# Layer 2 of a decoder: softmax sums and mask in three bf16 parts instead of fp32

## The chip, the cores and the metric

The kernel runs on one core of one Trainium2 chip. It is one launch that computes a whole four-layer decoder. The metric is device time in microseconds (us); lower is better. A core has a matmul engine (TensorE, PE in the profile, with its weight loads listed apart as PEld), VectorE (DVE), ScalarE (ACT), GpSimd (POOL), and SyncE (SP), whose queue issues nearly all DMAs here. Matmuls read their two operands from SBUF and write to PSUM[...].

## What is computed

The reference takes x of 4 x 512 tokens with 128 features and a context of 4 x 77 tokens, and applies four layers of self attention, cross attention and a feed-forward block, each as `x = x + block(layernorm(x))`. The change touches two blocks of layer 2:

```python
# cross attention (4 heads of 32), context tokens masked
logits = where(mask, MASK_FILL, q @ k.T)        # MASK_FILL = -2.3819763e38
# "ffn": attention of 16 heads of 64 whose values and outputs are mixtures of 8 experts
gv, go = gate(x, Wsel_v), gate(x, Wsel_o)       # sigmoid, the 2 best of 8 experts
v   = einsum('bsd,bhse,hedp->bhsp', x, gv, Wv)
att = softmax(einsum('bhsp,bhtp->bhst', q, k) / sqrt(64))
o   = einsum('bhst,bhtp->bhsp', att, v)
out = einsum('bhsp,bhse,hepd->bsd', o, go, Wo)
```

followed by a dense block with two layer norms. All inputs are fp32.

## The kernel before, in words

Matmuls are written through `dot` (line 421), which issues one product for each pair it is given and adds them in PSUM. An fp32 product of up to 512 columns stands in the trace as two MATMUL instructions, a bf16 product as one. `tt` (line 432) is VectorE's two-operand operation; everything that goes through it has that line in the profile, so such groups are told apart by tile names.

**The attention of layer 2's third block** is `l2_ffn`. It makes 32 passes, one for each of 4 batches and 8 pairs of heads, over PSUM tag `mm` with 7 banks. A pass t is three lists of steps:

- `attend(t)`: four row tiles of scores (`score`), each exponentiated on ScalarE with the row sums accumulated into `den` (128 x 4 x 2: query row, row tile, head of the pair); the exponentials turned by TensorE, 8 transposes for each row tile (`turn`, line 1795); then `turn_sums`, which inverts `den` on VectorE (line 1800), turns it with four fp32 transposes (line 1803) into a 2 x 512 PSUM tile and copies that on ScalarE to `dT` (line 1805); then `values`, 16 half-width instructions of the attention times v (line 1812) into `po`, and one product of `pick` (2 x 128, row h is one in the 64 columns of head h) with `dT`, which spreads the inverted sums over 128 partitions, and `po` is scaled with it on VectorE (the group `mm<-oT,mm`).
- `finish(t-1)`: the output experts of the pass before (groups `og<-mm,c` on VectorE and line 1845 on TensorE).
- `project(t+1)`: queries, keys, their rotation, and gated values (groups `roped`, `rot`, `gvx`) for the next pass.

`emit` puts the steps of the second and third list between those of the first, in proportion to the weights that stand beside the steps of `attend`. The passes are in turn woven with a second chain by `weave`: in rounds 0 to 14 the layer-2 attention, cross attention and gates of batches 2 and 3 (one step of the chain for every 3.3 steps of the passes), in rounds 15 to 30 the dense block of batches 0 and 1 (one for every 9), at the end that of batch 2. This program order is what the source gives; the framework that builds the kernel then orders each engine's queue by its own estimates, so a VectorE instruction may stand some places earlier or later in its queue than in the source. Waits between engines are semaphores that it sets.

**The cross attention of layer 2** is `l2_context` (once) and `l2_xattn` (for each batch). `l2_context` loads one row of the mask, and makes `fill`, a row of 4 x 77 fp32 values that are zero or MASK_FILL (lines 1542 to 1549). `score(j)` in `l2_xattn` adds two products in PSUM: queries times keys, 308 columns, and a product of a row of ones (1 x 128) with `fill`, repeated for four heads, which adds the mask to all 128 rows (lines 1611 to 1615). There are 16 of these, four for each batch. Those of batches 0 and 1 run beside the second half of layer 1's experts, those of batches 2 and 3 beside the passes of `l2_ffn`.

**Two helpers that are there already** and that the change calls: `in_three` (line 1281) splits an fp32 tile into three bf16 parts with four VectorE operations, the last of which gives the third part; `turned3` (line 1291) turns such a tile with four bf16 transposes and copies it on ScalarE. Layer 0 uses both for its own sums, with 48 columns, and has similar operations with 12 columns at lines 1151 to 1163.

Of the kernel before, what the change touches and what calls it, by code (L numbers as in the profile page):

```python
# [13 lines left out]
F32 = mybir.dt.float32  # L14
BF16 = mybir.dt.bfloat16
I32 = mybir.dt.int32
U8 = mybir.dt.uint8
AF = mybir.ActivationFunctionType
ALU = mybir.AluOpType
# [3 lines left out]
P = 128  # L23
B, S, D = 4, 512, 128
NT = B * S // P
TB = S // P
L = 77
BIG = 1.0e30
PAD = -3.0e38
FILL = -2.3819763e38  # L30
# [36 lines left out]
def rep(v):  # L67
    v = np.asarray(v).reshape(1, -1)
    return np.broadcast_to(v, (P, v.shape[1]))
# [35 lines left out]
def in_parts(a, n):  # L105

    out = []
    for _ in range(n):
        out.append(a.astype(ml_dtypes.bfloat16))
        a = a - out[-1].astype(np.float32)  # L110
    return out
# [19 lines left out]
def pack_all(inp):  # L131
    f32 = np.float32
# [3 lines left out]
    p = packs["const"] = Pack()  # L136
    p.add("tri8", rep((np.arange(8)[None, :] < np.arange(8)[:, None]).astype(f32)))
    p.add("tri4", rep((np.arange(4)[None, :] < np.arange(4)[:, None]).astype(f32)))
    p.add("place", ((np.arange(TB)[None, :, None] * P + np.arange(P)[:, None, None]) * 4 + np.arange(4)).astype(f32))
    p.add("slot1", rep((np.arange(32) * CAP + 1).astype(f32)))  # L140
    p.add("upper", (np.arange(P)[:, None] < np.arange(P)[None, :]).astype(f32))
    hd = np.arange(P) // 8
# [8 lines left out]
    one, zero = np.ones((32, S), f32), np.zeros((32, S), f32)  # L151
# [4 lines left out]
    p = packs["l0_attn.qk"] = Pack()  # L156
# [9 lines left out]
    p = packs["l0_attn.vo"] = Pack()  # L166
# [9 lines left out]
    p = packs["s1"] = Pack()  # L176
# [15 lines left out]
    p = packs["s2"] = Pack()  # L192
# [19 lines left out]
    p = packs["s3"] = Pack()  # L212
# [3 lines left out]
    turn = np.concatenate([np.arange(16, 32), np.arange(16)])  # L216
# [20 lines left out]
    for hp in range(8):  # L237
        h = slice(2 * hp, 2 * hp + 2)
        p = packs[f"l2_ffn.qkv{hp}"] = Pack()
# [3 lines left out]
        p = packs[f"l2_ffn.o{hp}"] = Pack()  # L243
        p.add("o", inp["L2_ffn_Wo"][h].transpose(0, 2, 1, 3).reshape(P, 8, D))
    p = packs["s4"] = Pack()
# [18 lines left out]
    p = packs["s5"] = Pack()  # L264
    p.add("gate_bias", rep(inp["L3_ffn_bias"]))
    p = packs["s5.gate"] = Pack()
# [23 lines left out]
class Net:  # L290
# [7 lines left out]
    def __init__(self, ctx, tc, packs, dram, feed):  # L298
        self.tc, self.nc = tc, tc.nc
        self.packs, self.dram = packs, dram  # L300
        self.feed, self.loaded = feed, []
        self.stay = {}
        self.turn = 0
        self.last = []
        self.chunks, self.sums = {}, {}
        nc = self.nc
        pool = lambda name, bufs, **kw: ctx.enter_context(tc.tile_pool(name=name, bufs=bufs, **kw))
        self.keep = pool("keep", 1)
        self.wpool = pool("weights", self.SLOTS)
        self.small = pool("small", 4)  # L310
        self.away = pool("away", 1, space=bass.MemoryType.DRAM)

        k = self.keep
        self.x = k.tile([P, NT, D], F32, name="x")
        self.xn = k.tile([P, NT, D], F32, name="xn")
        self.xT = k.tile([P, NT * P], F32, name="xT")
        xin = dram["x"].rearrange("(t p) d -> p t d", p=P)
        fetch = lambda b: nc.sync.dma_start(self.x[:, TB * b : TB * b + TB, :], xin[:, TB * b : TB * b + TB, :])
        fetch(0)
        self.want(0)  # L320
        self.const = self.load("const", k, "const")
        self.want(1)
        for b in range(1, B):
            fetch(b)
        self.ident = k.tile([P, P], F32, name="ident")
        make_identity(nc, self.ident)
        self.ones = k.tile([P, P], F32, name="ones")
        nc.gpsimd.memset(self.ones, 1.0)
        self.identb = k.tile([P, P], BF16, name="identb")
        nc.vector.tensor_copy(self.identb, self.ident)  # L330

        self.causal = k.tile([P, P], BF16, name="causal")
        nc.gpsimd.memset(self.causal, 0.0)
        nc.gpsimd.affine_select(
            out=self.causal, in_=self.causal, pattern=[[-1, P]], compare_op=ALU.is_ge,
            fill=-BIG, base=0, channel_multiplier=1,
        )
# [1194 lines left out]
    def l2_context(self, W, pool, work):  # L1532


        nc = self.nc
        H = 4
        one = lambda shape, name: pool.tile(shape, F32, tag=name, name=name, bufs=1)
        temp = lambda shape, name: work.tile(shape, F32, tag=name, name=name, bufs=2)
        s1 = one([P, 1], "s1")
        nc.vector.tensor_scalar(s1, W["rms"], 1.0, None, ALU.add)  # L1540

        mask8 = pool.tile([1, B * L], U8, name="mask8", bufs=1)
        nc.sync.dma_start(mask8, self.dram["mask"][0:1, :])
        fill = one([1, B * L], "fill")
        for a in "q", "qr":
            nc.vector.tensor_scalar(W[a], W[a], s1, None, ALU.mult)
        yield
        nc.vector.tensor_copy(fill, mask8)
        nc.vector.tensor_scalar(fill, fill, 1.0, -FILL, ALU.subtract, ALU.mult)
        ctx = self.const["ctx"].rearrange("l (b d) -> l b d", b=B)  # L1550
        mv = self.moments(lambda b: ctx[:, b, :], B, self.small, "rc")[:L]
        yield
        ms, rc = one([L, B], "ms"), one([L, B], "rc")
        self.tt(ms, mv[:, :, 0], mv[:, :, 0], ALU.mult)
        self.tt(ms, ms, mv[:, :, 1], ALU.add)
        self.rsqrt(rc, ms, 1e-6)
        yield
        cn = temp([L, B, D], "q")
        self.tt(cn, ctx, rc.unsqueeze(2).to_broadcast([L, B, D]), ALU.mult)
        yield  # L1560
        pt = self.sm()
        for b in range(B):
            nc.tensor.transpose(pt[:, b * L : b * L + L], cn[:, b, :], self.ident[:L, :L])
        cT = temp([P, B * L], "k")
        nc.vector.tensor_scalar(cT, pt[:, : B * L], s1, None, ALU.mult)
        yield
        t1, t2 = temp([P, B, L], "v"), temp([P, B, L], "e4")
        view = lambda ps: ps[:, : B * L].rearrange("p (b l) -> p b l", b=B)
        kb, vo = one([P, B, H, L], "kb"), one([L, H, B, D], "vo")
        self.x2 = kb, vo, fill  # L1570
        nc.gpsimd.memset(kb, 0.0)
        for t, w, c in ((t1, "k", "cosk"), (t2, "kr", "sink")):
            ps = self.sm()
            self.dot(ps[:, : B * L], (W[w], cT))
            self.tt(t, view(ps), W[c].unsqueeze(1).to_broadcast([P, B, L]), ALU.mult)
            yield
        for h in range(H):
            r = slice(32 * h, 32 * h + 32)
            self.tt(kb[r, :, h, :], t1[r], t2[r], ALU.add)
        yield  # L1580
        pv = self.sm()
        self.dot(pv[:, : B * L], (W["v"], cT))
        vT = temp([P, B * L], "q")
        nc.scalar.copy(vT, pv[:, : B * L])
        yield
        for h in range(H):
            r = slice(32 * h, 32 * h + 32)
            po = self.sm((P, B, D))
            for b in range(B):
                self.dot(po[:L, b, :], (vT[r, b * L : b * L + L], W["o"][r, :]))  # L1590
            self.move(vo[:, h], po[:L])
            yield

    def l2_xattn(self, b, W, pool, n):
        nc = self.nc
        H = 4
# [12 lines left out]
        def score(j):  # L1609
            s = self.sm((P, H, L))  # L1610
            self.dot(
                s,
                (q[:, j * P : j * P + P], kb[:, b]),
                (self.ones[0:1, :], fill[:, b * L : b * L + L].unsqueeze(1).to_broadcast([1, H, L])),
            )
            return self.less_maxima(s, H, pool, 2 * n)

# [75 lines left out]
    def l2_ffn(self, pool, gv, y, away, passes, feed, wants):  # L1693
# [5 lines left out]
        E = 8  # L1699
        n = len(passes)  # L1700

        pick = pool.tile([2, 2, 64], F32, name="pick")
        nc.gpsimd.tensor_copy(pick, self.ident[:2, :2].unsqueeze(2).to_broadcast([2, 2, 64]))

        other = pool.tile([P, 2, S], F32, name="rot")
        nc.gpsimd.memset(other, 0.0)
# [55 lines left out]
        def attend(t):  # L1762
# [28 lines left out]
            def turn(i):  # L1791
                for hl in range(2):
                    p = self.mm((P, TB, P))
                    for j in range(TB):
                        nc.tensor.transpose(p[:, j, :], es[i][hl][:, j * P : j * P + P], self.ident)  # L1795
                    nc.scalar.copy(eT[hl][:, :, i * P : i * P + P], p)  # L1796

            def turn_sums():
                spread(0)
                nc.vector.reciprocal(den, den)  # L1800
                p = self.mm((2, S))
                for i in range(TB):
                    nc.tensor.transpose(p[:, i * P : i * P + P], den[:, i, :], self.ident)
                m["dT"] = pool.tile([2, S], F32, tag="dT", name="dT")
                nc.scalar.copy(m["dT"], p)

            def values():
                spread(1)
# [14 lines left out]

            return [
                (lambda: score(0, 1), 4), (lambda: turn(0), 1), (lambda: score(2, 3), 1), (lambda: turn(1), 2),
                (lambda: turn(2), 2), (lambda: turn(3), 2), (turn_sums, 1), (values, 4),
            ]

        def finish(t):
# [546 lines left out]
```

## Time and profile before

| what | value |
|---|---|
| median of 3 runs | 2305.12 us (2304.5 to 2309.32) |
| the profiled execution | 2308.67 us |
| its span in the profile | 2306.8 us |
| PE busy, of the span | 94% |
| DVE busy, of the span | 69% |
| ACT busy, of the span | 45% |
| POOL busy, of the span | 24% |
| stretch of the 32 passes | from about 913 to 1917 us |
| granted clock of TensorE in that stretch | 1.00 |

The profiled execution is 3.55 us above the median. Its span leaves 1.9 us of the execution outside. Matmul records overlap each other[...]: a 512-column fp32 instruction is shown as 592 ns long, but the next starts 429 ns after it. What an instruction costs TensorE is therefore read from starts, not from its duration. A timeline line joins instructions of one group that follow each other; the cost of such a line is the start of the next line less its own.

### The profile page before, as it was taken

What the parts mean: (1) busy time and instruction counts of PE and PEld (TensorE: products, weight loads), DVE (VectorE), ACT (ScalarE), POOL (GpSimd) and SP (SyncE); (2) the same over time, 40 slices, a digit from 0 to 9 for tenths busy, and PEclk for the clock granted to TensorE, in tenths of its full rate; (3) what the DMA queues carried; (4) which work ended last, traced back from release to release, by engine and by line L of the source; (5) the groups of instructions that cost most, each with busy time, mean ns of one, the idle gap of its engine ahead of it and who ended that gap; (6) DMA issues with size and microseconds to landing.
All of it is one profiled execution on the core that took longest, in us unless ns stands there. A gap on an engine that the chain in (4) does not pass through costs nothing. (4 is left out here: it accounts for less than half of the span.)

```text
span 2306.8 us, 28326 instructions
## 1 busy us (share of the span) xinstructions
PE 2164.1 (94%) x9154; PEld 1142.8 (50%) x9154; DVE 1600.5 (69%) x4027; ACT 1027.8 (45%) x2102; POOL 556.6 (24%) x693
## 2 busy tenths in 40 slices
PE   6999899999999998999999999999999999498878
PEld 3566556554545553444444444444444444465553
DVE  6666576566675779777967696767776765686636
ACT  4555446444325462544444344444444444165432
POOL 1000001000000002333323333333333332335552
PEclk8988899999999999999999999999999999799779
DMA  6321134153453344233333344333333334200022
GB/s 165 99 61 43 45 108 132 51 141 104 110 148 90 90 103 117 59 94 94 92 85 82 87 113 108 103 103 94 103 103 94 82 99 101 92 1 6 1 71 75
DMA packets 81774, 204.72 MB, mean 89 GB/s; under 512 B 18799, under 2 KB 37551, under 8 KB 81371
## 3 DMA queue, kind: packets, MB, share of 16 engines
q1 hardware_dynamic: 78058, 198.99, 32.2%
q0 software_dynamic: 3568, 3.93, 0.6%
q8 instruction: 72, 1.18, 0.2%
q14 instruction: 76, 0.61, 0.1%
HBM read 173.94 MB, written 23.40 MB: 86 GB/s over the span
## 5 line engine op out<-in xcount | busy, mean ns | idle before, releaser
L1756 POOL TENSOR_TENSOR gvx<-gvx 128x512 f32<-128x512 f32 (+1 forms) x256 | 259.8, 1015 | 583.7 <-DVE gvx L432 528.6
L421 PE MATMUL f<-xT,w_l_ffn 128*128 128x512 f32 (+1 forms) x768 | 367.9, 601 | 1.2 <-ACT h L1001 0.7
L1876 ACT ACTIVATE at_e<-mm,at_m 128x512 f32<-128x512 f32 x256 | 172.8, 685 | 215.3 <-DVE at_m L1874 209.6
L421 PE MATMUL mm<-w_l_ffn_qkv,xT 128*128 128x512 f32 x512 | 265.5, 603 | 3.3 <-DVE roped L1727 1.7
L1845 PE MATMUL mm<-og,w_l_ffn_o 128*128 128x512 f32 x512 | 264.6, 600 | 0.0
L432 DVE TENSOR_TENSOR h<-h,f 128x512 f32<-128x512 f32 (+1 forms) x192 | 131.3, 685 | 136.1 <-PE f L421 110.3
L1001 ACT ACTIVATE h<-f 128x512 f32<-128x512 f32 x189 | 112.4, 596 | 249.7 <-PE f L421 217.2
L421 PEld LDWEIGHTS f<-xT,w_l_ffn 128*128 128x128 f32 (+1 forms) x768 | 139.5, 191 | 149.0 <-issue 126.1
L1009 PE MATMUL acc<-h,w_l_ffn 128*128 128x512 f32 x378 | 193.4, 596 | 3.5 <-DVE h L432 2.9
L432 DVE TENSOR_TENSOR og<-mm,c 128x512 f32<-128x512 f32 x256 | 175.8, 688 | 29.0 <-PE mm L1845 27.6
L432 DVE TENSOR_TENSOR gvx<-mm,gv 128x512 f32<-128x512 f32 x256 | 174.3, 683 | 23.6 <-PE mm L421 18.9
L1796 ACT COPY eT<-mm 128x512 f32<-128x512 f32 x256 | 137.5, 595 | 73.3 <-PE mm L1795 73.0
L1874 DVE TENSOR_REDUCE at_m<-mm 128x1 f32<-128x512 f32 x256 | 161.2, 683 | 8.9 <-PE mm L421 7.2
L1795 PEld LDWEIGHTS mm<-ident,at_e 128*128 128x128 f32 x1024 | 120.1, 141 | 67.0 <-issue 49.5
L1845 PEld LDWEIGHTS mm<-og,w_l_ffn_o 128*128 128x128 f32 x512 | 89.4, 191 | 97.0 <-issue 85.3
L1795 PE MATMUL mm<-ident,at_e 128*128 128x128 f32 x1024 | 134.1, 273 | 2.6 <-ACT at_e L1876 2.6
L421 PE MATMUL mm<-roped 64*128 64x512 f32 x512 | 133.4, 623 | 1.5 <-DVE roped L432 1.0
L421 PEld LDWEIGHTS mm<-w_l_ffn_qkv,xT 128*128 128x128 f32 x512 | 86.7, 190 | 91.9 <-issue 69.4
L1139 DVE TENSOR_REDUCE m<-mm 128x1 f32<-128x512 f32 (+3 forms) x176 | 105.3, 637 | 35.5 <-PE mm L1135 34.7
L1812 PE MATMUL mm<-eT,v 128*64 128x512 f32 x512 | 119.5, 599 | 0.0
L1009 PEld LDWEIGHTS acc<-h,w_l_ffn 128*128 128x128 f32 x378 | 70.9, 191 | 92.9 <-issue 66.9
L432 DVE TENSOR_TENSOR h<-h,c 128x512 f32<-128x512 f32 x160 | 111.1, 700 | 3.9 <-DMA c<-l_ffn_w 1.1
(457 smaller groups left out, 3646.3 us busy)
## 6 DMA issues: line engine op xcount, KB each, us to landing
c<-gates SPq DMA_DIRECT2D x256, 256.0 KB
c<-l_ffn_w SPq DMA_DIRECT2D x96, 384.0 KB
w_l_ffn<-in_l_ffn SPq DMA_DIRECT2D x26, 576.0 KB
w_l_ffn_qkv<-in_l_ffn_qkv SPq DMA_DIRECT2D x16, 640.0 KB
w_l_ffn_o<-in_l_ffn_o SPq DMA_DIRECT2D x16, 512.0 KB
rot<-qk SPq DMA_DIRECT2D x128, 64.0 KB
k_parts<-k SPq DMA_DIRECT2D x12, 384.0 KB
qs<-q_parts SPq DMA_DIRECT2D x48, 96.0 KB
```

The costliest lines, as they stand in the source:

```text
L421: self.nc.tensor.matmul(out, lhsT=lhsT, rhs=rhs, start=i == 0, stop=i == len(pairs) - 1)
L432: self.nc.vector.tensor_tensor(out, a, b, op)
L1001: nc.scalar.activation(h, pg, AF.Silu)
L1009: nc.tensor.matmul(acc["t"], lhsT=W["d" + u], rhs=h, start=i == 0, stop=i == n - 1)
L1139: nc.vector.tensor_reduce(m[:, i, h0 : h0 + per], ps, AX.X, ALU.max, negate=True)
L1756: nc.gpsimd.tensor_tensor(x[:, :, :m], x[:, :, :m], x[:, :, m : 2 * m], ALU.add)
L1795: nc.tensor.transpose(p[:, j, :], es[i][hl][:, j * P : j * P + P], self.ident)
L1796: nc.scalar.copy(eT[hl][:, :, i * P : i * P + P], p)
L1812: nc.tensor.matmul(po[64 * hl : 64 * hl + 64, :], lhsT=m["v"][:, j, hl, :], rhs=eT[hl][:, j, :], start=j == 0, stop=j == TB - 1,)
L1845: nc.tensor.matmul(acc, lhsT=W["o"][:, (e - 1) * D : e * D], rhs=hs.pop(e - 1), start=e == 1, stop=e == E)
L1874: nc.vector.tensor_reduce(m, s, AX.X, ALU.max, negate=True)
L1876: nc.scalar.activation(e[:, :n], s, AF.Exp, bias=m, accum_out=den)
```

## The change

The softmax sums of `l2_ffn` are inverted in a step of their own, `invert`, that stands between `turn(1)` and `turn(2)` with weight 0, and there they are also split into three bf16 parts with `in_three`. `turn_sums` turns the parts with `turned3`: four bf16 transposes of 6 columns in place of four fp32 ones of 2 columns, and a 6 x 512 copy in place of a 2 x 512 one. `pick` becomes a bf16 tile of 6 rows, each head's row three times, so that the spreading product is one bf16 product over 6 rows that adds the three parts. In the cross attention MASK_FILL is split into three bf16 parts on the host (one more column, `fill`, in the `const` pack), the mask is loaded in three rows, and the mask's product is a bf16 product over 3 rows of ones.

```diff
@@ pack_all
+    parts = in_parts(np.array([FILL], f32), 3)
+    p.add("fill", -np.concatenate(parts).astype(f32).reshape(3, 1))
@@ Net.__init__
+        self.onesb = k.tile([3, P], BF16, name="onesb")
+        nc.gpsimd.memset(self.onesb, 1.0)
@@ l2_context
-        mask8 = pool.tile([1, B * L], U8, name="mask8", bufs=1)
-        nc.sync.dma_start(mask8, self.dram["mask"][0:1, :])
-        fill = one([1, B * L], "fill")
+        mask8 = pool.tile([3, B * L], U8, name="mask8", bufs=1)
+        nc.sync.dma_start(mask8, self.dram["mask"][0:3, :])
+        mask, fill = one([3, B * L], "mask"), pool.tile([3, B * L], BF16, name="fill", bufs=1)
...
-        nc.vector.tensor_copy(fill, mask8)
-        nc.vector.tensor_scalar(fill, fill, 1.0, -FILL, ALU.subtract, ALU.mult)
+        nc.vector.tensor_copy(mask, mask8)
+        nc.vector.tensor_scalar(fill, mask, 1.0, self.const["fill"], ALU.subtract, ALU.mult)
@@ l2_xattn, score
-                (self.ones[0:1, :], fill[:, b * L : b * L + L].unsqueeze(1).to_broadcast([1, H, L])),
+                (self.onesb[0:3, :], fill[:, b * L : b * L + L].unsqueeze(1).to_broadcast([3, H, L])),
@@ l2_ffn
-        pick = pool.tile([2, 2, 64], F32, name="pick")
-        nc.gpsimd.tensor_copy(pick, self.ident[:2, :2].unsqueeze(2).to_broadcast([2, 2, 64]))
+        rows = pool.tile([6, 2], F32, name="own_rows")
+        pick = pool.tile([6, 2, 64], BF16, name="pick")
+        nc.gpsimd.tensor_tensor(rows, self.ident[:6, 0:2], self.ident[:6, 2:4], ALU.add)
+        nc.gpsimd.tensor_tensor(rows, rows, self.ident[:6, 4:6], ALU.add)
+        nc.gpsimd.tensor_copy(pick, rows.unsqueeze(2).to_broadcast([6, 2, 64]))
@@ l2_ffn, attend
+            def invert():
+
+                nc.vector.reciprocal(den, den)
+                m["d3"] = pool.tile([P, TB, 3, 2], BF16, tag="d3", name="d3")
+                self.in_three(m["d3"], den, pool, "d_rest")
+
             def turn_sums():
                 spread(0)
-                nc.vector.reciprocal(den, den)
-                p = self.mm((2, S))
-                for i in range(TB):
-                    nc.tensor.transpose(p[:, i * P : i * P + P], den[:, i, :], self.ident)
-                m["dT"] = pool.tile([2, S], F32, tag="dT", name="dT")
-                nc.scalar.copy(m["dT"], p)
+                m["dT"] = self.turned3(m.pop("d3"), pool)
...
-                (lambda: turn(2), 2), (lambda: turn(3), 2), (turn_sums, 1), (values, 4),
+                (invert, 0), (lambda: turn(2), 2), (lambda: turn(3), 2), (turn_sums, 1), (values, 4),
```

The helpers that it calls:

```python
    def in_three(self, out, w, pool, tag):
        nc = self.nc
        r, n = w.shape[1], w.shape[2]
        rest = pool.tile([P, r, n], F32, tag=tag, name=tag)
        nc.vector.tensor_copy(out[:, :, 0, :], w)
        self.tt(rest, w, out[:, :, 0, :], ALU.subtract)
        nc.vector.tensor_copy(out[:, :, 1, :], rest)
        self.tt(out[:, :, 2, :], rest, out[:, :, 1, :], ALU.subtract)

    def turned3(self, parts, pool):
        nc = self.nc
        n = 3 * parts.shape[3]
        t = self.bank("mm", [n, S], BF16)
        for j in range(TB):
            nc.tensor.transpose(t[:, j * P : j * P + P], parts[:, j].rearrange("p k n -> p (k n)"), self.identb)
        out = pool.tile([n, S], BF16, tag=f"turned{n}", name="turned", bufs=1)
        nc.scalar.copy(out, t)
        return out
```

## The prediction

> **What bounds the kernel now.** I read the page's busy shares first, then the same shares stretch by stretch, then TensorE's timeline inside one pass, since only starts tell its cost.
>
> ```profile
> PE 2164.1 (94%) x9154; PEld 1142.8 (50%) x9154; DVE 1600.5 (69%) x4027; ACT 1027.8 (45%) x2102; POOL 556.6 (24%) x693
> ...
> core 0: us, PE busy (x) PEld busy (x) DVE busy (x) ACT busy (x) POOL busy (x), PEclk, DMA share, GB/s
> 1403.00:1489.00 86.00, 86.00 (x326) 39.10 (x322) 63.79 (x114) 36.68 (x87) 29.35 (x36) 1.00 0.41 111
> 913.00:1403.00 490.00, 480.50 (x1880) 229.87 (x1878) 376.01 (x726) 218.04 (x500) 172.54 (x208) 1.00 0.35 91
> 690.00:913.00 223.00, 216.89 (x706) 109.78 (x705) 162.07 (x434) 104.49 (x164) 15.06 (x24) 0.99 0.37 97
> ```
>
> Three clean passes (1403 to 1489) have PE busy in every microsecond, DVE in 74%. In the passes woven with other work PE is at 98%, in the stretch with layer 1's last experts at 97%, at full clock. PE's queue sets the time in both places that the change touches. The waits of the clean passes say the same:
>
> ```profile
> engine line waited for: us in total, times, longest us
> ...
> DVE mm L432 <- PE mm L421: 15.3, 3, 5.2
> ```
>
> Once a pass DVE stands about 5 us at `mm<-oT,mm` for the product with `pick`: DVE waits for PE there. The timeline of PE (start, length, then the group; cost is start to start):
>
> ```profile
> 1196.49 1.02 PE L421 MATMUL mm<-w_l_ffn_qkv,xT 128*128 128x512 f32 x2
> 1197.35 1.02 PE L421 MATMUL s<-q,k 128*128 128x512 f32 x2
> 1198.21 0.60 PE L1803 MATMUL mm<-ident,den 128*2 128x128 f32 x4
> 1198.65 1.02 PE L1845 MATMUL mm<-og,w_l_ffn_o 128*128 128x512 f32 x2
> 1199.60 3.65 PE L1812 MATMUL mm<-eT,v 128*64 128x512 f32 x16
> 1203.19 1.12 PE L421 MATMUL mm<-dT,pick 2*128 2x512 f32 x2
> 1204.24 1.12 PE L421 MATMUL mm<-w_l_ffn_qkv,xT 128*128 128x512 f32 x2
> 1205.20 1.02 PE L1845 MATMUL mm<-og,w_l_ffn_o 128*128 128x512 f32 x2
> ```
>
> A full-array fp32 product costs 0.86 us (1196.49 to 1197.35). The product with `pick` costs 1.05, and the one after it 0.96: whenever the shape in use changes between full array, few rows and few columns, the instruction before is followed 0.09 us late (L1845 before L1812: 0.95), and the next fp32 product loses 0.10. The fp32 transposes with 2 columns cost 0.44 together and show no such loss.
>
> **What the Trainium skill says.** "TensorE: Matmul & The Clock Gate", section "Wait — 56ns, not 53.3ns?", gives 55.6 and 215.7 ns from start to start for warm bf16 matmuls of 128 and 512 columns; the lines below agree. "TensorEngine Tiling (Array Packing)", section "Key Properties", says that changing the tiling mode drains the array, which fits the 0.09 us; its section "Restrictions" says that column tiling disables the fp32 transpose mode, which fits that 2-column fp32 transposes pay no drain, and warns that bf16 ones may.
>
> **The change on PE, part by part.** What bf16 costs is shown in layer 0 and at the end of layer 3:
>
> ```profile
> 104.37 1.02 PE L421 MATMUL mm<-turned,pick 48*128 48x512 bf16 x4 [0.70 <-ACT turned L1299]
> 105.32 0.39 PE L1161 MATMUL mm<-identb,d 128*12 128x128 bf16 x4
> 105.64 0.39 PE L1132 MATMUL mm<-ks,qs 81*128 81x512 bf16 x1
> ...
> 2293.42 0.60 PE L421 MATMUL s<-w3T,pick 96*128 96x512 bf16 x2
> 2293.86 1.88 PE L421 MATMUL f<-xT,w_l_ffn 128*128 128x512 f32 x4
> ...
> 779.62 0.68 PE L421 MATMUL s<-kb,q 128*128 128x308 f32 x2
> 780.24 0.78 PE L421 MATMUL s<-fill,ones 1*128 1x308 f32 x2
> 780.95 0.79 PE L421 MATMUL s<-kb,q 128*128 128x308 f32 x2
> ```
>
> *Spreading product, 32 times.* Two bf16 products with 96 rows cost 0.44 (2293.42 to 2293.86), so 0.215 to 0.22 each, and going from fp32 to bf16 costs nothing in itself. Four with 48 rows cost 0.95: four times 0.215 and one drain of 0.09. Now: 0.09 before, 1.05, 0.10 on the next = 1.24. After, with 6 rows: 0.09 + 0.215 + 0.09 + 0.10 = 0.495. Gain 0.745, times 32 = 23.8 us. If 6 rows drained nothing, 0.215 would be left and the gain 32.8; no row shows so few rows in bf16, and the two fp32 products with 1 and 2 rows both pay, so I take 23.8.
>
> *Transposes, 32 x 4.* Now 0.44. The nearest row is the 12-column one: 0.32 for four (105.32 to 105.64), that is 4 x 0.056 and one drain of 0.09. Entering costs another 0.09, and the fp32 product after it, L1845, 0.10: 0.51. That is a loss of 0.07, 2.2 us in all. If 6 bf16 columns change no mode it is 0.22, a gain of 0.22 or 7.0 us. I take the loss, since the 12-column row drains and the fp32 exemption doesn't carry over.
>
> *Mask products, 16.* Now 0.71 (780.24 to 780.95), with the 0.09 of the drain into it and 0.10 on the next besides. At the bf16 rate 308 columns are 0.13, with the drain out of it 0.22; what lies on both sides stays. Gain 0.49, times 16 = 7.8 us, half of it beside layer 1's experts at 97% PE. Bounds: nothing there if DVE holds that stage (4 us), 9 if no drain is paid.
>
> Sum on PE: -23.8 + 2.2 - 7.8 = -29.4 us.
>
> **What it adds elsewhere.** `in_three` is four DVE operations a pass. The nearest rows:
>
> ```profile
> L432 DVE TENSOR_TENSOR d_rest<-m,d x16: 168/172/177, 40.4 to 255.4; 128x16 f32<-128x16 f32 x16
> L1153 DVE CAST d<-d_rest x16: 172/182/560, 40.6 to 256.0; 128x16 bf16<-128x16 f32 x16
> ```
>
> So 4 x 0.18 = 0.7 us a pass, 23 us in all, hidden by the 5 us that DVE stands once a pass; if that cover were gone it would cost all of it. The reciprocal already stands right behind the last exponential of its pass (0.12 us after it in clean passes), so `invert` adds hardly any wait. Queued behind it stand `rot`, `gvx`, `roped` and `og`. The tightest is the `og` that in one clean pass ran at 1452.45 and was used at 1455.79: 2.66 us of slack, of which 0.7 goes. The new hand-over is the third part, which must be ready for the transposes: in the built program it stands about eight places behind the reciprocal, after that `og`, so at about 1453.9, and PE reached the transposes at 1455.36. Some 1.1 us, allowing for the weight load ahead of them, is left in a clean pass, less where the woven chain puts more before it.
>
> The step `invert` also lengthens a pass from 27 steps to 28, so the woven chain advances 4% sooner. The order of the built program shows PE's queue in clean passes otherwise unchanged, some chain work a few places earlier, and ScalarE with four more table loads, between the sigmoids of the gates and the exponentials. One takes 1.283 us in this trace; the skill's "ScalarE activation tables: per-element evaluation and per-set limits", section "What a function is on this engine", has the same figure. ScalarE is busy 45%, and the exponentials are ready 2 us or more ahead of their transposes in 95 of 100 cases. For table loads, late parts and reshuffled chain I put 1.5 us, between -6 and +12: PE's idle gaps in the passes sum to some 20 us now, in a few pieces of up to 3 us, and a new order can mend or make such pieces.
>
> At nothing: the copy of 6 rows on ScalarE (12 rows took 574 ns as 2 rows do), the three GpSimd operations for `pick` (once, 40 us before use; 1.5 us if uncovered), the memset, the cast and scaling of the mask (0.3 us each as before; DVE works partitions in parallel), two more mask rows in one DMA, and one column more in 2244 of the `const` load, for which one DVE instruction waits 0.5 us at the start (under 0.05 us). SP's queue keeps its DMAs.
>
> Total: -29.4 + 1.5 = -28 us. The profiled execution would go from 2308.67 to about 2281; the median stood 3.55 us below it, so 2305.1 - 28 = 2277 us.
>
> **Rivals.** *A, small bf16 shapes cost no drain:* for it, the skill ties drains to tiling modes and nothing here shows 6 columns; against it, 12 columns and 48 rows both drain. Transposes gain 7.0 instead of losing 2.2, and the product may gain more: 2268, down to 2259 at most. *B, DVE and the reshuffled queues take back a good part:* DVE is at 77% in the woven stretch (376 of 490 us) and the change shortens PE's side while adding to DVE's. If half of the 32 passes lose 0.7 us, 11 us come back: about 2289. *C, slower:* the third part comes after PE reaches the transposes. PE takes its queue in order, so `values` would stand as well. It decides when PE waits over 29.4/32 = 0.92 us in every pass, so the part must come 2 us later than I place it (the 1.1 us of cover and 0.92); if it came 3 us later, 32 waits of 1.9 us would give 2338. Against it: DVE catches up before that in clean passes. *D, no gain:* a bf16 product of 6 rows is paced like fp32; the 0.95 for four of 48 rows speaks against it. Then some 2303.
>
> **How the numbers follow.** Forecast 0.68 (2271 to 2284), A 0.14, B 0.13, C 0.02, D 0.03. The predicted time is the forecast's, 2277. The range 2263 to 2290 takes in most of A and half of B. This kernel's measurement can tell about 0.2%, 4.6 us, from no change: faster 0.95, same 0.03, slower 0.02.
>
> **What would show it.** In the profile after: the line with `turned` and `pick` followed by the next product 0.3 us later (0.215 means A), that next product at 0.96; the four transposes of `d` at 0.32 with 0.09 before (0.22 means A); a clean pass 0.67 us shorter than 28.46 (1403.42 to 1431.88, from one product with `pick` to the next); mask products at 0.22; DVE's wait at `mm<-oT,mm` about 1.3 us shorter. PE waiting at the transposes for `d` would show C or B. The prediction is wrong if clean passes don't shorten, or if idle gaps of PE in the woven passes grow by more than 10 us.

## The result, and the profile after

| | before | after |
|---|---|---|
| median of 4 runs each, same chip | 2304.81 us (2299.01 to 2309.32) | 2279.88 us (2274.62 to 2285.02) |
| ratio after / before | | 0.9892, 95% interval 0.9871 to 0.9914 |
| the profiled execution | 2308.67 us | 2274.62 us |
| its span in the profile | 2306.8 us | 2272.5 us |
| first product of the mask, from the start of the span | 776.2 us | 764.8 us |
| from there to the end | 1530.6 us | 1507.8 us |

The kernel became 24.9 us faster (the interval makes that 20 to 30 us); the forecast was 28 us and 2277 us. The spans of the two profiled executions differ by 34.3 us, which is too much: 11.4 us of it lie ahead of the first product that the change touches. There the granted clock of TensorE differed. This view gives busy time of each engine by stretch, with PEclk, the granted clock, third from the end. First the kernel before, then the kernel after, each in layer 0:

```profile
30.00:282.00 252.00, 230.84 (x1858) 148.30 (x1857) 164.70 (x456) 137.55 (x264) 11.00 (x12) 0.88 0.25 68
```

```profile
30.00:280.00 250.00, 228.56 (x1886) 145.73 (x1886) 171.65 (x484) 141.42 (x274) 12.17 (x13) 0.93 0.26 70
```

That this is chance was seen later: two profiled executions of one and the same kernel (e4 and e8 below) reach that product at 774.1 and 765.2 us. From here on profiles are compared from the first product of the mask, where the mean granted clock is 0.97 or more up to the end of the passes. There the change brought 22.8 us.

The page's busy shares of the kernel after, and the same three stretches as before (three clean passes; the passes woven with other work; layer 1's last experts):

```profile
PE 2123.0 (93%) x9106; PEld 1119.3 (49%) x9106; DVE 1616.9 (71%) x4155; ACT 1031.7 (45%) x2106; POOL 554.7 (24%) x696
...
1375.00:1459.00 84.00, 84.00 (x321) 38.09 (x319) 64.77 (x126) 36.27 (x86) 29.34 (x36) 1.00 0.41 113
900.00:1375.00 475.00, 463.32 (x1854) 221.49 (x1852) 381.34 (x781) 222.40 (x503) 170.13 (x208) 1.00 0.35 94
677.00:900.00 223.00, 217.67 (x708) 109.80 (x707) 164.62 (x440) 105.01 (x166) 15.30 (x26) 0.98 0.36 98
```

TensorE still works through every microsecond of the clean passes, so there each nanosecond off its queue is a nanosecond off the end. In the woven stretch its share fell from 98.1% to 97.5% while VectorE's rose from 76.7% to 80.3%. In the clean passes VectorE's wait at the spreading product reads differently now:

```profile
DVE mm L436 <- ACT oT L1825: 14.5, 3, 4.8
```

What it costs on TensorE is read from starts (timeline: start, length, group):

```profile
1397.08 1.02 PE L425 MATMUL mm<-w_l_ffn_qkv,xT 128*128 128x512 f32 x2
1398.03 0.39 PE L1301 MATMUL mm<-identb,d 128*6 128x128 bf16 x4
1398.35 1.12 PE L1853 MATMUL mm<-og,w_l_ffn_o 128*128 128x512 f32 x2
1399.41 3.65 PE L1820 MATMUL mm<-eT,v 128*64 128x512 f32 x16
1402.99 0.39 PE L425 MATMUL mm<-turned,pick 6*128 6x512 bf16 x1
1403.31 1.13 PE L425 MATMUL mm<-w_l_ffn_qkv,xT 128*128 128x512 f32 x2
1404.27 1.02 PE L1853 MATMUL mm<-og,w_l_ffn_o 128*128 128x512 f32 x2
...
1430.79 0.39 PE L425 MATMUL mm<-turned,pick 6*128 6x512 bf16 x1
...
764.76 0.30 PE L425 MATMUL s<-fill,onesb 3*128 3x308 bf16 x1
764.99 1.98 PE L425 MATMUL f<-xT,w_l_ffn 128*128 128x512 f32 x4
```

The spreading product is followed after 0.32 us (1402.99 to 1403.31) where it was 1.05, and the next product still takes 0.96. The four transposes take 0.32 (1398.03 to 1398.35); the product ahead of them lasts 0.95 instead of 0.86, and the one behind them 1.06 (1398.35 to 1399.41), where it had 0.95 before. The clean pass is 27.80 us from product to product, 0.66 less. The mask's product takes 0.23 instead of 0.71.

### The profile page after: what moved, and what is told of

Same layout as the page of the kernel before. It is cut to its first block, busy times and chain, and to the rows that moved or that the text cites. A ratio compares the mean times of both kernels' runs of the same rounds, so it can differ in the third digit from the quotient of the medians.

```text
span 2272.5 us, 28370 instructions
## 1 busy us (share of the span) xinstructions
PE 2123.0 (93%) x9106; PEld 1119.3 (49%) x9106; DVE 1616.9 (71%) x4155; ACT 1031.7 (45%) x2106; POOL 554.7 (24%) x696
```

## The experiments

From starts alone, TensorE should have lost 29.4 us. Cut at fixed products (the first of the mask, the first, 15th and last spreading product), the three stretches up to the last spreading product went from 1139.5 to 1118.4 us, 21.1 less. The idle pieces of TensorE in them are the other part of the sum. I count a piece where a matmul starts over 0.25 us later than the columns of the one before it account for; they grew from 28.1 to 36.1 us. Arithmetic and pieces make -29.4 + 8.0 = -21.4, so they account for the 21.1. (The count is a rough one. In e2 below the pieces grow by 2.3 us while the stretches get 0.7 us shorter; and the stretches of the kernel after hold four more products of the dense block, 1.7 us, which run just ahead of the last spreading product there and just behind it in the kernel before.) The question is where the 8.0 us come from, for which the forecast's sum had 1.5. The theories:

- theory 1, the sum itself: drains around small shapes have the assumed size, and what is missing is not in them;
- theory 2, VectorE: the four added operations a pass were costed at nothing, and are not hidden everywhere;
- theory 3, the order: the step `invert` shifts the woven chain, and its new order has more waits;
- theory 4, pace: TensorE is now faster, so it meets VectorE and ScalarE sooner, whatever the edit.

A piece isn't always a wait. It can also be a matmul that takes twice as long, because the granted clock of TensorE falls to 0.50 for 3.4 us at a time; where TensorE is busy, each such stretch costs 1.7 us (the lines under e1 show one). The last two columns of the table keep the two apart for the passes alone, from the first spreading product to the last: TensorE's waits as the profile adds them up, and the number of stretches at half clock. These stretches go with the program: e4 and e8, one and the same kernel, have them at the same places of the passes to 0.1 us, and e7 and e9 have none there. What brings them on was not followed up.

| run | what it is | median us | ratio, 95% interval | first mask product to end | idle pieces | waits in the passes | at half clock in the passes |
|---|---|---|---|---|---|---|---|
| before | | 2301.8 to 2305.0 by group of runs | 1 | 1530.6 | 28.1 | 11.5 | 1 |
| after | | 2279.88 | 0.9892, 0.9871 to 0.9914 | 1507.8 | 36.1 | 17.5 | 1 |
| e1 | before + mask in bf16 | 2299.81 | 0.9986, 0.9965 to 1.0006 | 1527.6 | 31.3 | 12.0 | 3 |
| e2 | before + an empty step | 2302.35 | 0.9997, 0.9983 to 1.0012 | 1527.9 | 30.4 | 14.0 | 0 |
| e3 | before + the split, unused | 2303.62 | 1.0018, 1.0000 to 1.0036 | 1531.2 | 31.4 | 13.0 | 2 |
| e4 | after, small shapes widened | 2268.61 | 0.9856, 0.9818 to 0.9894 | 1492.3 | 36.9 | 19.2 | 2 |
| e5 | after, split in `turn_sums` | 2293.95 | 0.9961, 0.9950 to 0.9972 | 1517.8 | 50.3 | 26.6 | 3 |
| e6 | e4, split in `turn_sums` | 2279.14 | 0.9892, 0.9875 to 0.9908 | 1507.8 | 51.8 | 26.9 | 5 |
| e7 | e4, split on GpSimd | 2261.69 | 0.9835, 0.9805 to 0.9865 | 1486.4 | 33.2 | 14.4 | 0 |
| e8 | e4 again | 2268.79 | 0.9850, 0.9826 to 0.9874 | 1489.2 | | | |
| e9 | e7 again | 2264.43 | 0.9810, 0.9782 to 0.9838 | 1486.7 | | | |
| e10 | after, split on GpSimd | 2272.37 | 0.9856, 0.9831 to 0.9882 | 1504.0 | 31.3 | 13.2 | 0 |

(In e8 and e9 the record of one spreading product is missing, so their pieces aren't summed over the same stretches.)

**e1, the mask alone.** On the kernel before: the added column of `const`, three rows of the mask, and

```diff
-                (self.ones[0:1, :], fill[:, b * L : b * L + L].unsqueeze(1).to_broadcast([1, H, L])),
+                (self.onesb[0:3, :], fill[:, b * L : b * L + L].unsqueeze(1).to_broadcast([3, H, L])),
```

> The mask's bf16 products alone, on the kernel before. Theory 1 (what TensorE's queue saves is what the kernel saves): 16 x 0.48 = 7.7 us less from the first mask product to the end, half of it before the passes begin, each mask product 0.23 us from start to start. Theory 2 (the stretch beside layer 1's experts is held by another engine): only the half in the passes, 3.8 us.

The products went from 0.71 to 0.23 us as forecast. The stretch beside layer 1's experts, with 8 of the 16, fell by 3.6 us (169.11 to 165.52), nearly the 3.8 that 8 times 0.48 make. The stretches of the passes, with the other 8, gained 1.4 us up to the 15th product and lost 1.7 after it, while idle pieces rose by 3.0 us there. Nearly all of that rise is half clock, not waiting: the waits grew by 0.5 us, but two passes have a stretch at half clock that the kernel before has not. These two are the only passes that got longer, by 1.6 and 1.7 us. One of the stretches, in the view of busy time (PEclk third from the end), and two starts in it:

```profile
1813.90:1817.30 3.40, 3.40 (x9) 1.75 (x8) 3.40 (x7) 0.81 (x2) 0.27 (x1) 0.50 0.02 5
...
1814.63 1.91 PE L1849 MATMUL mm<-og,w_l_ffn_o 128*128 128x512 f32 x2
1816.34 1.51 PE L1799 MATMUL mm<-ident,at_e 128*128 128x128 f32 x8
```

The product that costs 0.86 us elsewhere takes 1.71 here. Without these two stretches, 3.3 us, the passes gained 3.0 of the 3.8 us. So TensorE's queue saves what the sum says in the passes too, and what takes it back in this kernel is the granted clock.

**e2, an empty step, and e3, the split alone.** Both on the kernel before. e2 puts a step that does nothing where `invert` stands; e3 puts `invert` there, with reciprocal and split, but nothing reads the three parts, and sums and mask stay fp32.

```diff
-(lambda: turn(2), 2), (lambda: turn(3), 2), (turn_sums, 1)
+(lambda: None, 0), (lambda: turn(2), 2), (lambda: turn(3), 2), (turn_sums, 1)   # e2
+(invert, 0), (lambda: turn(2), 2), (lambda: turn(3), 2), (turn_sums, 1)         # e3
```

> The kernel before with an empty step of weight 0 where invert stands: nothing is computed otherwise, only the woven chain moves ahead by one step in 28. Theory 3 (the shifted chain makes the new idle pieces of TensorE): 4 to 8 us slower than before, with idle pieces in the passes beside the dense block. Theory 2 (VectorE's four added operations make them): no change within 2 us.

> The kernel before with invert as a step and the split into three parts, whose result nothing reads; transposes and spreading product stay fp32. It adds VectorE's 23 us and the step, and takes nothing from TensorE. Theory 2: 6 us or more slower than before and slower than the empty step alone by 4 us or more. Theory 3: like the empty step alone, within 2 us of it. If both are hidden: within 2 us of before.

The empty step adds 2.3 us of idle pieces, and 2.5 us of waits in the passes, yet the three stretches are 0.7 us shorter (1138.8). In them are the same four products of the dense block, 1.7 us more work, and one stretch at half clock less, which is worth 1.7 as well. So the chain's new order makes TensorE wait more often, but as a whole it is worth nothing either way. The split makes the three stretches 2.8 us longer than the empty step does (1141.6), but e3 has two stretches at half clock in the passes, 3.4 us, where e2 has none, and its waits are no longer. So on the kernel before, where nothing waits for the parts, the 24.7 us that the operations take are hidden.

**e4, the drains taken away.** The kernel after with every small bf16 shape filled up with zeros to the full array: the parts go to columns 0 to 5 of zeroed tiles of 128 columns, four transposes of 128 columns, a `pick` of 128 rows with 122 of zeros, and 128 rows of ones against a `fill` with 125 rows of zeros.

```diff
-                m["d3"] = pool.tile([P, TB, 3, 2], BF16, tag="d3", name="d3")
-                self.in_three(m["d3"], den, pool, "d_rest")
+                m["d3"] = wide[t % 2]                    # two [P, TB, P] tiles, zeroed once
+                self.in_three(wide[t % 2][:, :, :6].rearrange("p j (k n) -> p j k n", k=3), den, pool, "d_rest")
...
-        pick = pool.tile([6, 2, 64], BF16, name="pick")
+        pick = pool.tile([P, 2, 64], BF16, name="pick")  # zeroed, then rows 0 to 5 as before
...
-                (self.onesb[0:3, :], fill[:, b * L : b * L + L].unsqueeze(1).to_broadcast([3, H, L])),
+                (self.onesb, fill[:, b * L : b * L + L].unsqueeze(1).to_broadcast([P, H, L])),
```

> The changed kernel with its small bf16 shapes filled up with zeros to the full array: transposes of 128 columns, spreading and mask products over 128 rows. If the 0.09 and 0.10 us around small shapes come from the change of shape, the transposes cost 0.22 with nothing on either side (0.29 less), the spreading product 0.22 with 0.05 before it (0.24 less), a mask product 0.13 (0.28 less): 32 x 0.53 + 16 x 0.28 = 21 us less than the changed kernel. If they come from going between fp32 and bf16, no change from the changed kernel.

The timeline of TensorE in e4, the same places as above:

```profile
1394.72 1.02 PE L425 MATMUL mm<-w_l_ffn_qkv,xT 128*128 128x512 f32 x2
1395.58 0.39 PE L1821 MATMUL mm<-identb,wide 128*128 128x128 bf16 x4
1395.81 1.08 PE L1864 MATMUL mm<-og,w_l_ffn_o 128*128 128x512 f32 x2
1396.81 3.65 PE L1831 MATMUL mm<-eT,v 128*64 128x512 f32 x16
1400.40 0.39 PE L425 MATMUL mm<-turned,pick 128*128 128x512 bf16 x1
1400.63 1.02 PE L425 MATMUL mm<-w_l_ffn_qkv,xT 128*128 128x512 f32 x2
1401.48 1.02 PE L1864 MATMUL mm<-og,w_l_ffn_o 128*128 128x512 f32 x2
...
774.11 0.30 PE L425 MATMUL s<-fill,onesb 128*128 128x308 bf16 x1
774.24 1.88 PE L425 MATMUL f<-xT,w_l_ffn 128*128 128x512 f32 x4
```

A product over 128 rows, 122 of them zeros, is 0.09 us cheaper than one over 6 (0.23 to 0.32), and the product behind it is back at 0.85. Four transposes of 128 columns take 0.23 where four of 6 took 0.32, with nothing lost ahead of them (0.86 for the product there); the one behind them takes 1.00, where the expectation had 0.95. The mask's product takes 0.13. So the losses come with the shape that differs from its neighbours, not with going from fp32 to bf16: theory 1 holds, and the sum was right to charge drains. A clean pass is 27.37 us. By these starts e4 should gain 0.43 us a pass and 0.30 for each mask product over the kernel after, 18 us; its three stretches gained 16.0, with idle pieces 0.8 larger. Most of the arithmetic arrives here.

**e5 and e6, the step taken out again.** The kernels after and e4, with `invert` no longer a step of its own but called at the head of `turn_sums`. The woven chain is then back at the old count of steps.

```diff
-(invert, 0),
...
                 spread(0)
+                invert()
```

> The changed kernel with invert called at the head of turn_sums and no step of its own, so that the woven chain advances as in the kernel before; all else as in the changed kernel. TensorE's idle pieces over 0.25 us between the first mask product and the last spreading product sum to 28 us before, 36 in the changed kernel, 30 with the empty step alone, 31 with the unused split. Theory 3 (the shifted chain makes them): 31 or less, the stretch 5 us shorter than in the changed kernel. Theory 2 (VectorE's added operations, of which some are held while GpSimd works): still 35 or more. Theory 4 (a faster TensorE runs into the pace of VectorE and ScalarE where the chain is dense, whatever the order): still 35 or more.

> The same, on the kernel with small shapes filled up to the full array: invert at the head of turn_sums, no step of its own. Theory 3: idle pieces 31 or less, against 37 with the step, and the stretch 5 us shorter. Theories 2 and 4: 36 or more.

With the old count the kernels are slower, by 14 and 11 us in the medians, and idle pieces are at 50.3 and 51.8. That is no clean test of theory 3, because the edit also puts the split right ahead of its reader. TensorE's waits in the passes of e5 (engine and line; for whom; us in total, times, longest us) show what was bought with the step:

```profile
PE mm L1301 <- DVE d L436: 13.7, 15, 2.7
```

In half of the passes TensorE reaches the transposes before the third part is there, and waits up to 2.7 us. That is rival C's mechanism at its real price. The other waits of e5 sum to 12.9 us, near the 11.5 of the kernel before. In the kernel after, the same group and its largest neighbours read:

```profile
PE mm L1802 <- ACT at_e L1884: 3.7, 3, 1.4
PE mm L425 <- ACT at_e L1884: 3.0, 8, 0.7
...
PE mm L1301 <- DVE d L436: 1.3, 1, 1.3
```

One wait of 1.3 us for the third part, and several for exponentials.

**e7, and e8, e9, e10: the split moved off VectorE.** The four operations go to GpSimd, which is busy 24%; the reciprocal stays on VectorE. e7 does it on e4, e8 and e9 repeat e4 and e7 side by side on one chip, and e10 does it on the kernel after, nothing widened. The edit of e10:

```diff
-                self.in_three(m["d3"], den, pool, "d_rest")
+                out = m["d3"]
+                rest = pool.tile([P, TB, 2], F32, tag="d_rest", name="d_rest")
+                nc.gpsimd.tensor_copy(out[:, :, 0, :], den)
+                nc.gpsimd.tensor_tensor(rest, den, out[:, :, 0, :], ALU.subtract)
+                nc.gpsimd.tensor_copy(out[:, :, 1, :], rest)
+                nc.gpsimd.tensor_tensor(out[:, :, 2, :], rest, out[:, :, 1, :], ALU.subtract)
```

> The kernel with full-array shapes, with the four operations of the split on GpSimd instead of VectorE (the reciprocal stays). Theory 2: idle pieces fall from 37 to 31 or less, 6 us faster. Theories 3 and 4: no change within 2 us, or slower if the split, queued behind GpSimd's sums of the values, comes too late for the transposes.

> The kernel of e4 once more, so that it stands on the same chip beside the one with the split on GpSimd. Both theories: ratio 0.985 to 0.987, as in e4; its profile again has PE's idle pieces in the three stretches at 35 to 38 us if they belong to the program, and elsewhere if they differ from one execution to the next.

> The kernel of e7 once more, beside e8. If VectorE's added operations make the idle pieces: 5 to 8 us below e8, ratio 0.982 to 0.984, idle pieces in the passes again some 7 us less than e8's. If they are of other origin and e7's gain was chance: within 2 us of e8.

> The changed kernel with only the four operations of the split moved to GpSimd, nothing widened. If VectorE's added operations cost the changed kernel what was missing: 5 to 8 us below the changed kernel, ratio 0.985 to 0.987, idle pieces of PE in the three stretches 28 to 31 us. If the split comes too late from GpSimd, whose operations are longer and queue behind its own: PE waits at the transposes for the third part, and the ratio is 0.99 or more. If neither: the changed kernel's 0.989.

e10 is the clean test. TensorE's arithmetic is that of the kernel after; its idle pieces fell from 36.1 to 31.3 us, the three stretches from 1118.4 to 1113.1. Of these 5.3 us, 1.7 are the one stretch at half clock that the passes of the kernel after have and those of e10 have not; TensorE's waits in the passes fell by 4.3 us. The ratio of 0.9856 against 0.9892 would be 8 us; the intervals overlap, so I rest on the stretches and waits, which are alike in executions of one kernel: e4 and e8 agree within 0.03 us in each of the 30 passes, from spreading product to spreading product, that both records show. e9's passes, from first spreading product to the end, are 6.7 us shorter than e8's (1321.6 to 1328.3). Its lead by the medians, 4.4 us, is not certain. In the first stretch e7 and e9 are 4.1 us longer than e4 and e8. They have six pieces of 0.4 to 0.6 us at the first projections, four of which the kernel after has as well and e8 none. These are no waits: in e9 the granted clock is 0.50 there, from 918.4 to 925.2 us, and in e8 it is 1.00 at the same products. Half clock makes up some 2.7 of the 4.1 us. A wait of 0.6 us for the third part is GpSimd's.

What VectorE loses is seen best in one place, with the same order on TensorE in both kernels. VectorE and then GpSimd in the kernel after:

```profile
1571.71 1.17 DVE L1290 CAST d<-den 128x8 bf16<-128x8 f32 x1
1572.79 1.21 DVE L436 TENSOR_TENSOR roped<-roped,rot 128x1024 f32<-128x1024 f32 x1
1573.92 1.23 DVE L436 TENSOR_TENSOR d_rest<-den,d 128x8 f32<-128x8 f32 x1
...
1571.57 1.28 POOL L1936 TENSOR_TENSOR d_z<-d_z,w_s 128x512 f32<-128x512 f32 x1 [4.68 <-ACT d_z L491]
1572.93 2.20 POOL L1937 TENSOR_TENSOR d_z<-d_z,w_s 128x512 f32<-128x512 f32 x1
```

and TensorE's transposes there, in the kernel after and in e10:

```profile
1574.24 1.02 PE L425 MATMUL mm<-w_l_ffn_qkv,xT 128*128 128x512 f32 x2
1576.56 0.39 PE L1301 MATMUL mm<-identb,d 128*6 128x128 bf16 x4 [1.29 <-DVE d L436]
```

```profile
1574.33 1.02 PE L425 MATMUL mm<-w_l_ffn_qkv,xT 128*128 128x512 f32 x2
1575.28 0.39 PE L1301 MATMUL mm<-identb,d 128*6 128x128 bf16 x4
```

The cast of 8 columns took 1.17 us instead of its usual 0.17, and the subtraction 1.23 instead of 0.16. Each ends within 0.03 us of the end of a GpSimd operation (1572.88 and 1572.85; 1575.15 and 1575.13). Two operations of 0.33 us together became 2.4, the third part came late, and TensorE waited 1.29 us, which e10 doesn't. Small VectorE operations that took over 0.25 us more than the median of their group (and whose median is under 0.3 us) were 8 in the stretch from 760 to 1920 us before (5.4 us over their medians), 17 after (13.9 us), 12 in e10 (9.8 us). Of the 128 operations of the split, five were held.

What is left of the 8.0 us in e10, 3.2, fits the order, theory 3, better than the pace, theory 4. In the passes e10's waits are 1.7 us above those of the kernel before, and the empty step's are 2.5 above. Both kernels have the step, and with it four more table loads on ScalarE (72 in place of 68). In e1, where only the mask products got faster, the waits grew by 0.5. But e2's stretches did not get longer with its waits, and no run took the whole of the new pace without the step, so this part stays open.

The kernel of e7 and e9 is the fastest of all, some 41 us below the kernel before by the medians.

## Why the prediction was right, and where it was not

- **TensorE is the bound in both places**: right. A nanosecond off its queue came off the clean pass: 0.66 us, forecast 0.67.
- **Spreading product, gain 0.745 a pass**: right in each of its terms: 0.09 ahead, 0.315 for the product with its drain, 0.10 on the next. Rival A, no drain for few rows, fell: e4 shows what that would look like.
- **Transposes, loss 0.07 a pass**: right (0.32 for four, 0.09 ahead, 0.10 behind), against the choice of a gain that would have come without drains. The Trainium skill's "TensorEngine Tiling (Array Packing)", section "Key Properties", on which the choice leaned, says that a change of mode drains the array; e4, which removes the change of shape and with it the loss, agrees.
- **Mask products, gain 0.49 each**: right on TensorE (0.48). Where DVE was feared, beside layer 1's experts, the gain arrived. In the passes, where I expected it, the products got as much shorter, but in e1 two stretches at half clock, which the sum had no term for, took most of it back.
- **VectorE's wait 1.3 us shorter**: wrong. It went from 5.1 to 4.8 us a pass, and is now ended by ScalarE's copy `oT`. Shortening what TensorE does just ahead moved the wait to the next of the two things that the operation needs.
- **The split at nothing, hidden by the 5 us that VectorE stands**: this is the step that failed in size. Its duration was right (236 + 193 + 180 + 162 ns, 24.7 us in all, 23 forecast), and it is hidden in clean passes, which are all that I had looked at. In the passes 4.3 us of TensorE's waits go away when it leaves VectorE (e10). I had put single operations at 0.18 us, and not seen that one can be held over a microsecond behind GpSimd.
- **+1.5 us for late parts and reshuffled chain, from -6 to +12**: measured 8.0, inside its bounds. This is the mis-sized term of the sum: -29.4 + 8.0 in place of -29.4 + 1.5. In the passes TensorE's waits grew by 6.0 us, of which 4.3 go when the split leaves VectorE; the rest, 1.7, is no more than the empty step's 2.5. The idle time that the forecast started from was too high as well: from 913 to 1917 us TensorE is idle for 15.0 us before, not some 20. The stretch behind the passes ended 1.7 us sooner (391.1 to 389.4), by the four products of the dense block that moved ahead of it, and that makes the 22.8 us from the first product of the mask on; the median's 24.9 us agrees with that within its interval.
- **Rivals B, C and D**: B had the right place (VectorE and the queues take part back) and, with 11 us, about the right size. It took the plain 0.7 us in half of the passes; in the place shown it was two held operations in one pass instead. C did not happen, since `invert` stands early as a step of its own; with the split at the head of `turn_sums` it does, at 14 us in 15 waits. D fell with the first timeline.

## What to carry to other kernels

Price a matmul from start to start, with what it takes from the ones around it; where TensorE is the bound and its gaps are few, such a sum comes out to about ten nanoseconds a pass. Before a late matmul is called a wait, look at the granted clock: e1's lost gain looked like waiting and was half clock. A small operand next to full-size products can cost more than the same one filled up with zeros, so widen it before trying to make it smaller. Look for the cover of added VectorE work in the most crowded passes and at what GpSimd does there, not in the clean ones, and put the work a few steps ahead of its reader: the same four operations brought some 14 us of waits when they stood right before it.

## What was not expected

VectorE and GpSimd hold each other up. "GPSIMD Engine Reference", section "Specifications", says that GpSimd's SBUF interfaces are shared with VectorE, with contention for VectorE operations with two SBUF inputs or in a two-port mode. The traces fit it, with sizes: an 8-column cast or subtraction of 0.16 us took up to 1.23 us beside a GpSimd operation over 512 columns, and in the place shown the GpSimd operation that started beside `roped` took 2.20 us where the one before it took 1.28. On GpSimd, whose durations are rough in the profile, the last operation of the split took 0.20 us at best and 1.12 in the median (group of e10; shortest, median, longest ns, first and last start):

```profile
L1814 POOL TENSOR_TENSOR d<-d_rest,d x32: 201/1118/1122, 929.1 to 1864.6; 128x8 bf16<-128x8 f32 x32
```

Which of the two it is goes with what VectorE runs beside it. In the first pair below the operation takes 1.12 us beside `roped`, whose two inputs both lie in SBUF, in the second 0.20 us beside an operation that reads PSUM:

```profile
1142.27 1.22 DVE L436 TENSOR_TENSOR roped<-roped,rot 128x1024 f32<-128x1024 f32 x1
1142.43 1.12 POOL L1814 TENSOR_TENSOR d<-d_rest,d 128x8 bf16<-128x8 f32 x1
...
1115.44 0.68 DVE L436 TENSOR_TENSOR og<-mm,c 128x512 f32<-128x512 f32 x1
1115.65 0.20 POOL L1814 TENSOR_TENSOR d<-d_rest,d 128x8 bf16<-128x8 f32 x1
```

So it is with all 32: the 19 that took 1.12 us stand beside `roped` or `rot` and end 0.06 us after it, the 11 of 0.20 us started beside operations that read PSUM, and two of about 0.6 us stand beside others with both inputs in SBUF. That agrees with what the page says of two SBUF inputs. The held cast on VectorE has one input, and whether it ran in a two-port mode the trace does not say; that the shared interface is what holds them was not tested by itself. The other surprise is layer 0: with the same program the first product of the mask came 8.9 us later in one execution than in another, at a granted clock of 0.89 against 0.91 between 30 and 280 us, while the 30 passes behind it repeated to hundredths of a microsecond.
